# Token stage: the Silus of its input projection move into the scan stage, and its group norm's Silu becomes Exp and Ln

## The chip, the cores and the metric

The kernel runs on one core of a Trainium2 chip. The metric is the device time of one execution in microseconds (us), the median of several runs. The engines named are PE (TensorE, matmuls; its weight loads are shown apart as PEld), DVE (VectorE), ACT (ScalarE), POOL (GpSimd) and SP (SyncE, which here issues all DMA transfers). A line such as L470 is a line of the kernel's file before the change, unless the text says otherwise.

## The reference, cut to what matters

The input is a batch of 64 images of 128 channels and 28 x 28 pixels, f32. Four layers follow one another:

- a quantized block of two 3x3 convolutions with batch norms over the whole batch;
- an attention over the 784 pixels of each image;
- a state space layer ("mamba") along the 784 pixels of each image, with 160 inner channels and 24 states, whose result is fused into the image: this image is called x2 below;
- a second, small state space layer on each pixel alone: the 128 channels of a pixel are 8 tokens of 16, and the recurrence runs over the 8 tokens. A group norm over 4 groups of channels and a Silu follow, and x2 is added.

The last layer is what the change touches. Shortened:

```python
seq = x.transpose(0, 2, 3, 1).reshape(B * H * W, 8, 16)
xz = seq @ in_proj_w.T                          # 16 -> 2 * 32
xi, z = split(xz, 2)
xs = silu(conv1d(xi, conv_w) + conv_b)          # causal, over the tokens
dt, Bm, Cm = split(xs @ x_proj_w.T, [1, 17])
dt = softplus(dt @ dt_proj_w.T + dt_proj_b)
h_t = exp(dt_t * A) * h_{t-1} + dt_t * Bm_t * xs_t      # 8 steps, 32 x 16 states
y_t = sum over the states of h_t * Cm_t
y = (y + xs * D) * silu(z)
out = x + silu(groupnorm(y @ out_proj_w.T))
```

Both silu(conv1d(..)) and silu(z) depend on x2 of the pixel alone. Because the convolution over tokens is linear, in_proj and convolution together are one 128 x 256 matrix on the 128 channels (`wxc`, with `cbT` as bias), and z is another (`Wz`).

## The kernel before, in words

The kernel is written for a framework that orders the instructions of each engine ahead of time, by the order in which they are written and by its own estimate of when each can start. Each engine then runs its list in that order; semaphores between engines hold the data dependencies. When the activation table that ACT has in place does not hold the function of the next ACTIVATE, an ACT_TABLE_LOAD stands before it. Silu is in another table than Exp and Ln.

There are three stages.

The conv stage (`conv_block`) goes over the batch twice and leaves its result in DRAM.

The scan stage (`attention_and_mamba`) takes the images one by one. For image b, `scan` runs 30 steps (24 of part A, with all 128 partitions one channel each, and 6 of part B, with 32 channels and four states at a time). A step is: ACT's Exp gives `a` (L464); PE broadcasts a row of B over the partitions into `bc` (`product`, L240); DVE multiplies by it (L469), scans along the pixels (L470) and multiplies by the broadcast row of C (L473); PE sums into `y` (L475). `a` has three buffers, `bc` has two in PSUM, and `y` has one. Between the steps, `run` draws pieces of side work from the generator `beside`: first the end of image b-1 (`after`: output projection, the four copies that undo the permutation, L497 to L502, the fusion product and x2 at L507, which is stored into `x2d`), then the beginning of image b+1 (`before`: query, key, value, attention, layer norm, input projection, convolution, and delta). Each `yield` ends a piece. All products of side work use one PSUM buffer, `side`, of two banks (`side_psum`), so each waits until the one before has been read. The delta of the next image ends on POOL: L445, L446 and L448, which gives `du`, read by L469.

The token stage (`token_mamba`) takes groups of G = 14 times 128 pixels (28 groups; an image is 784 pixels, so a group holds 2.29 images). A group has two halves (`dh`, 16 inner channels each) and a half has four blocks of four channels. For a group:

- `silus(k)` loads x2 in chunks of up to 512 pixels (`xch`), multiplies by `wxc` and `Wz` (L679), applies Silu out of PSUM (the tile `s`, two buffers) and stores to `utd` and `ztd` in DRAM. `use` puts a table load before and one after. It is called for group k+1 in the second block of group k's first half, and for group 0 ahead of everything.
- `x_proj(k)` reads `utd` back (`rows`), multiplies (L706), and DVE copies the result to `BC` (L716); L723 and L726 form the sums over B times C.
- `delta_u(k, dh)` computes the softplus (ACT: Abs, Exp, Ln; DVE: L768 to L770; POOL: L773, L774) and, at L777, `diag`.
- `exps` makes the 64 Exps of a block, the tile `a` with two buffers, on ACT.
- `block` runs the recurrence: POOL makes the inputs (`inject`, L807) and two products (L818, L820); DVE makes the first sum (L819, into PSUM) and then, step by step, L822, L824 and L826; PE sums over the states (L829 to L833), and ACT copies the result to `ysb`.
- `gate` multiplies by silu(z) (DVE L849, POOL L850), projects (L858), and collects whole images in `xr` (L868).
- `image_stats` computes mean and variance of an image's groups of channels (L639 to L654), and `image_end` applies the Silu with scale and bias and adds x2 on POOL (L662). Since it is a Silu, it waits for the next call of `silus`, so that it shares its table.

ACT's activations of the token stage are all written through the helper `act` and show the line L609.

Of the kernel before, what the change touches and what calls it, by code (L numbers as in the profile page):

```python
# [15 lines left out]
F32 = mybir.dt.float32  # L16
# [25 lines left out]
PK4 = dict(Wz=256, BDx=512, BDt=16, BDo=256, dtw=32, dtb=32)  # L42
PK4_TMP = dict(P1=256, P2=256, Alog=512)
# [12 lines left out]
PK4_AT, NPK4 = columns(PK4)  # L56

# [9 lines left out]
def tile_kernel(ctx: ExitStack, tc: tile.TileContext, x, w1t, w2t, m2t, vecs, pk3, pk4, out):  # L67
# [18 lines left out]

    c2d, s2, b2x15 = conv_block(tc, cpool, dram, x, w1t, w2t, m2t, v, eps)
    attention_and_mamba(tc, x, c2d, s2, b2x15, x2d, pk3, vec, v, ident, eps)
    token_mamba(tc, x2d, pk4, v, ident, eps, out, NB)
# [117 lines left out]
def attention_and_mamba(tc, x, c2d, s2, b2x15, x2d, pk3, vec, v, ident, eps):  # L207
# [6 lines left out]
    with ExitStack() as ctx:  # L214
# [41 lines left out]
        nc.vector.tensor_copy(inb[:32, 3:4], inb_ps[:32, 0, 3:4])  # L256

# [228 lines left out]
        def after(b, given, ys):  # L486
# [21 lines left out]
            nc.sync.dma_start(x2d[b], x2)  # L508

# [25 lines left out]
        for _ in after(NB - 1, given.pop(NB - 1), ys):  # L535
            pass


def token_mamba(tc, x2d, pk4, v, ident, eps, out, NB):
# [14 lines left out]
    SET = "natural_log_exp_and_others"  # L554
# [3 lines left out]
    with ExitStack() as ctx:  # L558
        dram = ctx.enter_context(dram)
        wp = ctx.enter_context(tc.tile_pool(name="w4", bufs=1))  # L560
        wxc = wp.tile([C, 256], F32, name="wxc")
# [3 lines left out]
        with tc.tile_pool(name="w4t", bufs=1) as tp:  # L565

            pt = tp.tile([C, 1024], F32, name="pt")
            nc.sync.dma_start(pt, pk4[:, NPK4:])
            nc.vector.tensor_mul(wxc, pt[:, 0:256], pt[:, 256:512])
            nc.scalar.activation(A, pt[:, 512:1024], AF.Exp)  # L570
            nc.vector.tensor_scalar(A, A, -1.0, None, ALU.mult)
# [21 lines left out]

        utd = [dram.tile([C, 2, PX], F32, name=f"utd{i}") for i in range(2)]
        ztd = [dram.tile([C, 2, PX], F32, name=f"ztd{i}") for i in range(2)]
# [3 lines left out]
        side = dict(load=None, since=[])  # L599

        def behind(ins, others):
            for o in others:
                tc.add_manual_dep(
                    ins.ins, o.ins.name,
                    mybir.DependencyInfo(mybir.DependencyClass.NoSync, mybir.DependencyReason.DATA), reason="table",
                )

        def act(*args, **kw):
            ins = nc.scalar.activation(*args, **kw)  # L609
            if args[2] in (AF.Exp, AF.Ln, AF.Silu):  # L610
                if side["load"] is not None:
                    behind(ins, [side["load"]])
                side["since"].append(ins)

        def use(name):
            ins = nc.scalar.preload_act_table_set(name)
            behind(ins, side["since"] or [side["load"]] if side["load"] is not None else side["since"])
            side["load"], side["since"] = ins, []
# [4 lines left out]
        def load_x(k, g, n):  # L623

            lo, hi = k * PX + g * C, k * PX + (g + n) * C
            xch = cp.tile([C, 512], F32, name="xch", bufs=2)
            for b in range(lo // T, (hi - 1) // T + 1):
                p, q = max(lo, b * T), min(hi, (b + 1) * T)
                nc.sync.dma_start(xch[:, p - lo : q - lo], x2d[b][:, p - b * T : q - b * T])
            return xch  # L630

        xr, done = {}, []
        affine = {}

        def image_stats(b):
            xo = xr[b]
# [18 lines left out]
            affine[b] = sm  # L655

        def image_end(b):
            xo, sm = xr.pop(b), affine.pop(b)
            res = p1.tile([C, T], F32, name="res")
            nc.sync.dma_start(res, x2d[b])  # L660
            act(xo, xo, AF.Silu, bias=sm[:, 7:8], scale=sm[:, 5:6])
            nc.gpsimd.tensor_tensor(res, res, xo, ALU.add)  # L662
            nc.sync.dma_start(out[b], res)

        def silus(k):

            use("silu_and_others")
            for b in done:
                image_end(b)
            done.clear()  # L670
            if k >= NGRP:
                return
            for g, n in chunks:
                m = n * C
                xch = load_x(k, g, n)
                for dst, weight, bias in ((utd, wxc, "cbT"), (ztd, w("Wz"), None)):
                    for dh in range(2):
                        acc = bank()
                        nc.tensor.matmul(  # L679
                            acc[:, :m], lhsT=weight[:, dh * C : (dh + 1) * C], rhs=xch[:, :m], start=True, stop=True  # L680
                        )
                        s = cp.tile([C, 512], F32, name="s", bufs=2)
                        act(s[:, :m], acc[:, :m], AF.Silu, **(dict(bias=v(bias, dh)) if bias else {}))
                        nc.sync.dma_start(dst[k % 2][:, dh, g * C : g * C + m], s[:, :m])

        def load_rows(src, k, dh, g, n):
            t = cp.tile([C, 512], F32, name="rows", bufs=4)
# [203 lines left out]
        for q, (k, dh) in enumerate(halves_):  # L891
# [4 lines left out]
            for i in range(NBLK):  # L896

                take(ends, 2)
                if dh == 0:
                    if i == 1:  # L900
                        take(ends, 9)
                    elif i > 1:
                        take(group_next, 3)
# [115 lines left out]
```

## Time and profile before

The median of 3 runs is 19954.88 us (19948.64 to 19957.86); the profiled execution has a span of 19946.5 us.

| | busy us in the span | share |
|---|---|---|
| PE | 15221.5 | 76% |
| DVE | 15317.0 | 77% |
| ACT | 10216.1 | 51% |
| POOL | 6488.5 | 33% |

The page counts an f32 matmul as two matmul instructions. The scan stage runs from about 1100 us to 12860 us, the token stage's first block starts at 12970.3 us. A wait is written as the instruction that waited and, after the arrow, the instruction that ended the wait. An engine's idle time only costs where something waits for that engine in turn.

The rows of the page that the change removes, moves or has a likeness for:

| row | count | mean ns |
|---|---|---|
| L679 PE, products of `silus` | 896 | 592 to 627 |
| L609 ACT, the Silus `s`, with and without bias | 448 | 629 and 543 |
| L616 ACT table load | 59 | 1283 |
| L716 DVE, copies to `BC` | 196 | 692 |
| L609 ACT, Silu of the group norm on 784 elements | 64 | 1038 |
| L662 POOL, sum with x2, 784 elements | 64 | 1852 |
| L464 ACT, Exp of a scan step | 1920 | 947 |
| L284 ACT, Silu of z in the scan stage | 128 | 908 |
| L443, L376 ACT, Ln and Exp from SBUF, 784 elements | 128, 64 | 857 |
| L470 DVE, scan | 1920 | 1930 |

### The profile page before, as it was taken

What the parts mean: (1) busy time and instruction counts of PE and PEld (TensorE: products, weight loads), DVE (VectorE), ACT (ScalarE), POOL (GpSimd) and SP (SyncE); (2) the same over time, 40 slices, a digit from 0 to 9 for tenths busy, and PEclk for the clock granted to TensorE, in tenths of its full rate; (3) what the DMA queues carried; (4) which work ended last, traced back from release to release, by engine and by line L of the source; (5) the groups of instructions that cost most, each with busy time, mean ns of one, the idle gap of its engine ahead of it and who ended that gap; (6) DMA issues with size and microseconds to landing.
All of it is one profiled execution on the core that took longest, in us unless ns stands there. A gap on an engine that the chain in (4) does not pass through costs nothing.

```text
span 19946.5 us, 166453 instructions
## 1 busy us (share of the span) xinstructions
PE 15221.5 (76%) x56424; PEld 8635.8 (43%) x56424; DVE 15317.0 (77%) x15223; ACT 10216.1 (51%) x22804; POOL 6488.5 (33%) x3000
## 2 busy tenths in 40 slices
PE   9978888888888887888888888666666666666666
PEld 5533333333333333333333333355555555555554
DVE  1367877787787778878778787688888888888887
ACT  0234444444444444444444443377777777777776
POOL 0010110111011011101101100177777777777776
PEclk9988888888888888888888888888888888888888
DMA  2400000000000000000000000011111111111111
GB/s 75 146 7 7 6 8 7 7 7 7 8 6 8 7 6 8 7 8 6 8 7 6 8 5 3 23 55 62 64 64 62 64 62 65 62 63 64 62 64 53
DMA packets 325636, 631.19 MB, mean 32 GB/s; under 512 B 39856, under 2 KB 103856, under 8 KB 324784
## 3 DMA queue, kind: packets, MB, share of 16 engines
q1 hardware_dynamic: 324784, 620.55, 9.5%
q8 instruction: 447, 7.32, 0.2%
q14 instruction: 405, 3.32, 0.1%
HBM read 389.20 MB, written 231.21 MB: 31 GB/s over the span
## 4 chain that ended last, share of the span: by engine, by line
PE 44%; DVE 30%; ACT 10%; POOL 9%; issue 6%; DMA 2%; SPq 0%; DVEq 0%; POOLq 0%; ACTq 0%
PE side L240 13%; PE y L475 10%; DVE h L470 8%; PE y L831 5%; PE acc L120 5%; ACT a L609 4%; DVE h L473 4%; POOL db L807 4%; PE side L340 4%; DVE h L469 3%; PE bc L240 2%; DVE h L822 2%; DVE a L824 2%; DVE h L826 2%; DVE cv L392 2%
## 5 line engine op out<-in xcount | busy, mean ns | idle before, releaser
L609 ACT ACTIVATE a<-delta,A 128x98 f32<-128x98 f32 x14336 | 3891.9, 366 | 822.4 <-PE y L831 687.4
L470 DVE TENSOR_TENSOR_SCAN h<-a,h 128x784 f32<-128x784 f32 x1920 | 3706.1, 1930 | 43.9
L807 POOL TENSOR_TENSOR db<-u,BC 128x896 f32<-128x896 f32 x1568 | 3285.5, 2109 | 774.4 <-DVE h L826 664.8
L464 ACT ACTIVATE a<-delta,A 128x784 f32<-128x784 f32 x1920 | 1818.6, 947 | 3125.4 <-DVE h L470 3047.3
L475 PE MATMUL y<-h,ident 128*128 128x392 f32 x6144 | 2879.6, 595 | 629.4 <-DVE h L473 623.3
L831 PE MATMUL y<-a,ident 128*128 128x280 f32 x7168 | 2157.9, 462 | 1453.5 <-DVE a L824 1449.1
L378 POOL TENSOR_TENSOR xn<-xc,lnv 128x784 f32<-128x784 f32 x64 | 124.1, 1938 | 8617.9 <-ACT lnv L376 8617.9
L831 PEld LDWEIGHTS y<-a,ident 128*128 128x128 f32 x7168 | 1576.9, 224 | 2020.8 <-POOL db L807 1145.5
L473 DVE TENSOR_TENSOR h<-h,bc 128x784 f32<-128x784 f32 x1920 | 1852.6, 965 | 335.5 <-PE bc L240 310.9
L240 PE MATMUL bc<-parts,sel 128*128 128x392 bf16 x7680 | 1946.9, 377 | 190.4 <-DVE h L469 190.1
L475 PEld LDWEIGHTS y<-h,ident 128*128 128x128 f32 x6144 | 1218.1, 219 | 1693.4 <-DVE h L473 990.5
L469 DVE TENSOR_TENSOR h<-du,bc 128x784 f32<-128x784 f32 x1920 | 1850.0, 964 | 32.9 <-PE bc L240 24.5
L240 PEld LDWEIGHTS <-sel 128*128 128x128 bf16 x7680 | 776.3, 110 | 1815.2 <-issue 1531.8
L822 DVE TENSOR_TENSOR h<-h,a 128x896 f32<-128x896 f32 x1344 | 1474.4, 1097 | 37.4
L826 DVE TENSOR_TENSOR h<-h,db 128x896 f32<-128x896 f32 x1120 | 1229.2, 1097 | 62.3 <-POOL db L807 0.9
L475 PE MATMUL y<-h,fold 128*32 128x392 f32 x1536 | 748.6, 621 | 448.8 <-DVE h L473 448.8
L824 DVE TENSOR_TENSOR a<-h,BC 128x896 f32<-128x896 f32 x896 | 975.7, 1089 | 24.6
L340 PE MATMUL side<-diag,e 112*112 112x112 f32 x6272 | 807.2, 288 | 155.7 <-DVE diag L335 155.7
L328 DVE TENSOR_REDUCE nmax<-side 112x1 f32<-112x784 f32 x448 | 436.7, 975 | 631.9 <-PE side L240 631.9
L340 PEld LDWEIGHTS side<-diag,e 112*112 112x112 f32 x6272 | 798.7, 204 | 271.2 <-issue 228.2
L833 PEld LDWEIGHTS y<-late,ident 128*128 128x128 f32 x7168 | 848.4, 193 | 48.9 <-issue 28.5
L833 PE MATMUL y<-late,ident 128*128 128x112 f32 x7168 | 845.0, 274 | 0.0
(194 smaller groups left out, 22390.3 us busy)
## 6 DMA issues: line engine op xcount, KB each, us to landing
rows<-utd SPq DMA_DIRECT2D x504, 256.0 KB, 2.8
utd<-s SPq DMA_DIRECT2D x168, 256.0 KB, 2.9
ztd<-s SPq DMA_DIRECT2D x168, 256.0 KB, 2.9
rows<-ztd SPq DMA_DIRECT2D x168, 256.0 KB, 2.9
xt<-in_x SPq DMA_DIRECT2D x32, 784.0 KB, 5.1
c1d<-raw SPq DMA_DIRECT2D x32, 784.0 KB, 6.2
xt<-c1d SPq DMA_DIRECT2D x32, 784.0 KB, 6.0
c2d<-raw SPq DMA_DIRECT2D x64, 392.0 KB, 4.4
```

Source lines behind the costliest of these rows:

```text
L240: nc.tensor.matmul(dst[:, h, :HT], lhsT=lhsT, rhs=rhs[:, h * HT : (h + 1) * HT], start=(i == 0), stop=(i == len(terms) - 1),)
L340: nc.tensor.matmul(tr[:, j // 4, (j % 4) * TP : (j % 4 + 1) * TP], lhsT=e[:, j * TP : (j + 1) * TP], rhs=diag, start=True, stop=True,)
L464: nc.scalar.activation(a, deltas[i], AF.Exp, scale=A[:, k : k + 1])
L469: nc.vector.tensor_tensor(halves(h), halves(dus[i]), bb[:, :, :HT], ALU.mult)
L470: nc.vector.tensor_tensor_scan(h, a, h, 0.0, ALU.mult, ALU.add)
L473: nc.vector.tensor_tensor(halves(h), halves(h), cc[:, :, :HT], ALU.mult)
L475: nc.tensor.matmul(y[:, hf, :HT], lhsT=red, rhs=h[:, hf * HT : (hf + 1) * HT], start=(j == 0), stop=(j == count - 1),)
L609: ins = nc.scalar.activation(*args, **kw)
L807: nc.gpsimd.tensor_tensor(x, of_dg(du[:, t, ds, :]), BC[:, t, :NS, :].unsqueeze(1).broadcast_to([C, DB, NS, G]), ALU.mult)
L822: nc.vector.tensor_tensor(h, h, flat(at(t)), ALU.mult)
L831: nc.tensor.matmul(y3[:, 1:6], lhsT=ident, rhs=a[:, 0:5, :, n, :], start=False, stop=False)
L833: nc.tensor.matmul(y3[:, 6:8], lhsT=ident, rhs=late[:, :, :, n, :], start=False, stop=(n == NS - 1))
```

## The change

The two products of the token stage's input projection, their Silus and the stores into `utd` and `ztd` are now done image by image in the scan stage: `after` appends them behind x2, as four products with one Silu and one store each, in two pieces that each end with a `yield`. `utd` and `ztd` become one DRAM tile for each image, and `load_rows` reads a chunk with one transfer, or with two where it crosses from one image to the next. `silus` and `load_x` are gone, and `x_proj` can read a group at any time.

The Silu of the group norm becomes Exp, Ln and Exp again: with v = scale * x + bias, silu(v) = v * exp(-ln(1 + exp(-v))). The three ACT instructions share the table with the others of the token stage. DVE computes v (one instruction), and POOL multiplies the two. It is now done in `finish_image`, in one go with the statistics and as a part of the generator `gate`, instead of at the next `silus`. The token stage thus keeps one table from its start: one load stands ahead of it. The draws of the pieces in the main loop change with it: the last block of a half now draws all of `gate` that is left, and `x_proj` of the next group is drawn by two pieces from the second block of the first half on, instead of by three from the third.

The core of the diff:

```diff
@@ attention_and_mamba, after
             nc.sync.dma_start(x2d[b], x2)
+            for dst, weight, bias in ((utd, wxc, "cbT"), (ztd, wz, None)):
+                for dh in range(2):
+                    acc = side_psum()
+                    product(acc, [(weight[:, dh * C : (dh + 1) * C], x2)])
+                    tok = tmp("tok")
+                    last[:] = [
+                        nc.scalar.activation(
+                            halves(tok), acc[:, :, :HT], AF.Silu, **(dict(bias=v(bias, dh)) if bias else {})
+                        )
+                    ]
+                    nc.sync.dma_start(dst[b][:, dh, :], tok)
+                yield
@@ token_mamba
-        def use(name):
-            ins = nc.scalar.preload_act_table_set(name)
...
+        load = nc.scalar.preload_act_table_set("natural_log_exp_and_others")
@@ finish_image (was image_stats and image_end)
+            nc.vector.tensor_scalar(sm[:, 0:1], sm[:, 5:6], -1.0, None, ALU.mult)
+            nc.vector.tensor_scalar(sm[:, 1:2], sm[:, 7:8], -1.0, None, ALU.mult)
             res = p1.tile([C, T], F32, name="res")
             nc.sync.dma_start(res, x2d[b])
-            act(xo, xo, AF.Silu, bias=sm[:, 7:8], scale=sm[:, 5:6])
+            e = p1.tile([C, T], F32, name="gate")
+            act(e, xo, AF.Exp, bias=sm[:, 1:2], scale=sm[:, 0:1])
+            act(e, e, AF.Ln, bias=1.0)
+            act(e, e, AF.Exp, scale=-1.0)
+            nc.vector.tensor_scalar(xo, xo, sm[:, 5:6], sm[:, 7:8], ALU.mult, ALU.add)
+            yield
+            nc.gpsimd.tensor_tensor(xo, xo, e, ALU.mult)
             nc.gpsimd.tensor_tensor(res, res, xo, ALU.add)
@@ load_rows
-            t = cp.tile([C, 512], F32, name="rows", bufs=4)
-            nc.sync.dma_start(t[:, : n * C], src[k % 2][:, dh, g * C : (g + n) * C])
+            t = cp.tile([C, 512], F32, name="rows", bufs=6)
+            for b in range(lo // T, (hi - 1) // T + 1):
+                p, q = max(lo, b * T), min(hi, (b + 1) * T)
+                nc.sync.dma_start(t[:, p - lo : q - lo], src[b][:, dh, p - b * T : q - b * T])
@@ main loop
                 take(ends, 2)
-                if dh == 0:
-                    if i == 1:
-                        take(ends, 9)
-                    elif i > 1:
-                        take(group_next, 3)
+                if i == NBLK - 1:
+                    take(ends, 99)
+                if dh == 0 and i > 0:
+                    take(group_next, 2)
                 take(nxt, 1)
...
-                if dh == 0 and i == 1:
-                    silus(k + 1)
-                    use(SET)
```

## The prediction

> **What bounds the kernel now.** I read first the span in slices (section 2 of the page), each digit the busy tenths of one 498.7 us slice. Up to slice 3 the conv stage runs, to slice 26 the scan stage, and from there the token stage.
>
> ```profile
> PE   9978888888888887888888888666666666666666
> DVE  1367877787787778878778787688888888888887
> ACT  0234444444444444444444443377777777777776
> POOL 0010110111011011101101100177777777777776
> ```
>
> No engine is full: the scan stage has PE and DVE near 8 tenths and ACT at 4; the token stage has DVE at 8, ACT and POOL at 7. Both stages are bound by waits in in-order queues. So I took one period of each, busy times by window (columns: window, length, then busy time of PE, PE loads, DVE, ACT, POOL):
>
> ```profile
> 6003.80:6188.40 184.60, 148.16 (x485) 69.73 (x484) 147.13 (x146) 77.17 (x95) 20.20 (x9) 0.87 0.02 7
> 15007.00:17010.00 2003.00, 1349.24 (x6290) 1039.93 (x6288) 1637.59 (x1579) 1458.36 (x4730) 1497.56 (x693) 0.83 0.20 63
> ```
>
> The first is one image of the scan stage: 184.6 us, DVE idle for 37. The second is some eight token groups. L723 runs once per group, from 12926.4 to 19551.7 us in 27 intervals: 245.4 us per group, so the 2003 us hold 8.16 groups. Per group that is DVE 200.7 busy and 44.7 idle, POOL 183.5, ACT 178.7, PE 165. What DVE waits for in 15000 to 17000 (total us, times, longest):
>
> ```profile
> DVE BC L716 <- PE bank L706: 182.2, 56, 10.5
> DVE h L819 <- POOL a L818: 75.8, 24, 6.9
> DVE xr L868 <- PE bank L858: 22.9, 12, 3.2
> ```
>
> Half of the idle time, 182.2 / 8.16 = 22.3 us per group, is one place. DVE's timeline there:
>
> ```profile
> 15031.70 1.09 DVE L824 TENSOR_TENSOR late<-h,BC 128x896 f32<-128x896 f32 x1
> 15039.99 0.69 DVE L716 COPY BC<-bank 128x512 f32<-128x512 f32 x1 [7.20 <-PE bank L706]
> ...
> 15058.99 0.69 DVE L716 COPY BC<-bank 128x512 f32<-128x512 f32 x1 [8.33 <-PE bank L706]
> ...
> 15061.73 3.91 DVE L777 TENSOR_TENSOR diag<-u,small 128x1792 f32<-128x1792 f32 x1
> 15065.56 2.82 DVE L819 TENSOR_TENSOR h<-a,db 128x896 f32<-128x896 f32 x1
> ```
>
> A block ends at 15032.8 and the next starts at 15065.6. ACT explains it:
>
> ```profile
> 15039.46 0.38 ACT L609 ACTIVATE s<-bank 128x256 f32<-128x256 f32 x1 [3.08 <-DMA utd<-s]
> 15039.86 1.28 ACT L616 ACT_TABLE_LOAD   x1
> 15041.16 1.70 ACT L609 ACTIVATE w<-w 128x1792 f32<-128x1792 f32 x1
> 15042.76 17.20 ACT L609 ACTIVATE a<-delta,A 128x98 f32<-128x98 f32 x64
> ```
>
> The 16 Silus of the next group stand together between two table loads, and their two buffers `s` wait for stores (99.2 + 54.3 us of ACT idle in these 2000 us, 18.8 per group). Only after the last may the 64 Exps of the next block run, 17.2 us, and the next group's x_proj (L706) cannot read `utd` before. The same delay returns as a wait of 6.88 us at the block at 15116.59 for POOL's L818, which waited for ACT's `a`.
>
> **What the skill says.** "ScalarE: Activation LUTs", section "What ACT_TABLE_LOAD costs": about 1283 ns and a drain of about 1380 ns. The trace has 1283 ns, and the next ACTIVATE starts 10 to 20 ns after; the drain is not seen apart, so I price a load at 1.28 us and take the page's 2.66 as the upper end. "PSUM — Partial Sum Buffer", section "Engine vs sequencer instructions": ScalarE, VectorE and GpSimd queues are strict FIFO and matmuls keep program order; the block waiting behind Silus agrees. "SBUF — State Buffer", section "SBUF: two separate sides": DVE instructions with two SBUF inputs and GpSimd instructions lock each other out; L819 (both inputs in SBUF) takes 1.10 us alone and 2.82 beside POOL, L470 1.79 and up to 3.48. So POOL work added to the token stage is not free for DVE.
>
> **The change, token stage.** Removed per group: 16 matmuls, 16 Silus, two loads, the `xch` reads and the `s` stores. In the changed program's DVE order the seven BC copies no longer stand in a row: they lie between operations of the group's last two blocks, with `rows` read from DRAM that the scan stage filled long before. The copies, L723 and diag (4.8 + 2.0 + 3.9 = 11 us of DVE) remain, the idle time between them has other work in it. I count off 22.3 us, and of the 9.3 per group at L819 the 6.9 after the Silus. ACT loses 16 x 0.58 + 2 x 1.28 = 12 us, which was beside DVE's work but for that gap.
>
> Added per image, 784 x 64 / 1792 = 2.29 images per group: Exp, Ln, Exp for one Silu of 1.04 us (rows of 857 ns for 784 elements: 2.6 us; net +1.6 ACT, hidden, since ACT has 178.7 - 12 + 3.6 = 170 of some 220 us); on DVE one 784 tensor_scalar (L296, same shape, 0.56) and two single-column ones (0.2 to 0.6, L653's 0.51 at the top): 1.0 x 2.29 = 2.2 us per group, on the path since DVE is the fullest; on POOL one product, 1.85 (L662): 4.2 us per group, making POOL 188. The new waits (DVE's affine behind ACT's first Exp; POOL's product behind Ln and Exp) I bound by 0 and by the ACT wait of the group norm today at three places, 3 x 1.7 x 2.29 = 12 us (L652 waits 1.7 at most); the order leaves several DVE operations between, so I take 3.
>
> Sum per group: -22.3 - 6.9 + 2.2 + 3 = -24, to 221.4; between -15 and -29. 27 groups have it: -650 us (-405 to -780). A check by blocks on the group that starts at 15065.56 and took 252.8 us, a long one: by the starts of L819, its four plain blocks take 22.3 to 24.7 us, the two with softplus 29.5 and 34.6, and the last two, with group norm, BC copies, L723 and diag added to 22.4 of block work, some 33 and 34: 226, or 27 less. silus(0) ran alone before the first block, 12887 to some 12920: -33.
>
> **The change, scan stage.** Added per image: 4 products of two f32 matmuls (the page counts each as two; one product 1.48 us in PE's timeline): 5.9 us PE; 4 Silus of 0.91. In the changed ACT order each stands alone between two `a` Exps, so each brings two loads: 4 x (2.57 + 0.91) = 13.9 us ACT. Program counts agree: 582 loads become 1021, 499 more after the token stage's 60 go. ACT had 77 of 184.6 us busy, so 91 fit. Behind a waiting Silu stand the `a` Exps, needed by DVE's scans (L470); behind a waiting product stand y and the bc broadcasts, because `side` has one buffer. Four stores per image, 1.6 MB, are some 9 GB/s.
>
> What moves: the products take one scan step each, directly after x2. Before, in the 50 us from the first delta product (6053.7) to the vt products (6104.0), four of image b's steps (B part) and four of b+1's lay; several were bare of side work, and DVE idled there:
>
> ```profile
> 6091.20 0.87 DVE L502 COPY r<-side 32x392 f32<-32x392 f32 x1 [5.41 <-ACT r L501]
> ```
>
> After, B's steps end some 3.5 earlier, eight of b+1's steps lie between, and the four new products fill them. I walked this stretch by the trace's durations in the new order. B's last y stands right behind the first delta product; then ACT's Abs, Exp, Ln with their loads and POOL's three products (L445, L446, L448: 1.84, 1.89 and 1.84 us at their shortest in this image) must end before DVE's first product of b+1: DVE idles 4 to 5 us, where before it idled 5.41 behind the yo product. The steps with a new product take 4.4 us by PE's chain (half y 0.74, product 1.48, half y 0.74, cc 0.42, DVE 0.97) against some 3.65 by DVE alone: four times 0.7. ACT needs 2.57 + 0.91 + 0.95 = 4.4 per such step and starts two `a` ahead: just hidden. Idle time thus stays about 11 us, vt comes 1 to 2 us later. Ends: -2 us per image (all in idle time and a shorter stretch before) and +5.9 (all PE work on the path). I take +1.5 x 63 = +95. The last image's four products have no scan beside them: 4 x 3.5 = 14 us.
>
> **Sum.** 19955 - 650 - 33 + 95 + 14 = 19381; I say 19380.
>
> **Rivals.** (1) ACT's table loads do reach DVE's scans, in full: +13.9 x 63 = 876 instead of 95: 20160, slower. For it: ACT's steps just fit, and side work is serial through one buffer. Against it: ACT waits 46.8 us per image for DVE's L470, that is, for buffers, not the reverse. (2) POOL becomes the token stage's bound: it is at 183.5 and gets 4.2 more, and near the end, with no side work, blocks still start 22.4 apart with 1.8 us waits for L818. If only 10 us per group are won: 19380 + 14 x 27 = 19760. (3) The products fill idle slots wholly and the stretch before shrinks: -2 x 63 in place of +95: 19160.
>
> **Numbers.** The forecast 0.64, (2) 0.14, (3) 0.12, (1) or half of it 0.10. The range takes (3) and the token bounds to 19100, and most of (2) to 19720. Faster by over 0.2% 0.88, within it 0.03, slower 0.09.
>
> **What would show it.** After: no table loads from some 13000 us on; no run of BC copies with waits on L706's successor; groups 215 to 230 us apart; DVE there at 9 tenths. Scan: 183 to 190 us per image, eight more loads in each, a wait of DVE for POOL's du at the image boundary. Wrong would be: images over 192 us with scans waiting for ACT's `a`, or groups over 235 with DVE waiting for POOL or for the group norm's Exp.

## The result and the profile after

The changed kernel takes 19391.79 us, median of 4 runs (19387.71 to 19407.3); the kernel before, in the same comparison, 19951.76 us. The ratio is 0.9724, with a 95% interval of 0.9707 to 0.974. The forecast was 19380 us, and the medians differ from it by only 12 us.

That closeness is luck: the total hides two misses of opposite sign and of the same size, 193 us each. The blocks gained 457 us where 650 were forecast, and the scan stage gained 98 where a loss of 95 was forecast. First and last starts of single lines cut the two profiled runs (spans 19946.5 and 19390.3 us) into stretches; the names of the lines are those of before, with the new line numbers after the stroke:

| stretch | before, us | after, us | difference | forecast |
|---|---|---|---|---|
| start to the first scan, L470 / L483 | 1116.6 | 1125.7 | +9 | 0 |
| first to last scan | 11740.2 | 11642.0 | -98 | +95 |
| last scan to last x2, L507 / L520 | 19.1 | 20.7 | +2 | 0 |
| last x2 to the first block, L819 / L811 | 94.4 | 80.5 | -14 | -33 + 14 = -19 |
| first to last block | 6904.5 | 6447.4 | -457 | -650 |
| last block to the end | 71.7 | 74.0 | +2 | 0 |

In the slices of the page after, a digit is again the busy tenths of one fortieth of the span:

```profile
PE   9978888888888888888888888866666666666666
DVE  1368878878788878888888887778888888888888
ACT  0235445445445445445445455457777777777776
POOL 0001101101101101101001011048888888888887
```

ACT in the scan stage went from 4 to between 4 and 5 tenths. In the token stage DVE now shows 8 throughout, where the forecast looked for 9, and POOL went to 8.

**Token stage.** L715 (was L723) runs from 12826.5 to 18981.7 us in 27 intervals: 228.0 us per group, from 245.4. The longest of DVE's waits between these two times (us in total, times, longest) follow; first of before, from 12926.9 to 19551.7 us:

```profile
DVE BC L716 <- PE bank L706: 618.3, 188, 13.8
DVE h L819 <- POOL a L818: 258.9, 78, 13.4
DVE xr L868 <- PE bank L858: 70.4, 38, 3.2
DVE yg L849 <- PE bank L844: 28.7, 26, 4.7
DVE yg L849 <- DMA rows<-utd: 6.1, 11, 2.0
```

and of after:

```profile
DVE h L811 <- POOL a L810: 233.0, 65, 13.4
DVE xr L860 <- PE bank L850: 184.3, 67, 6.4
DVE BC L708 <- PE bank L698: 62.5, 57, 2.0
DVE yg L841 <- PE bank L836: 60.2, 26, 5.0
DVE yg L841 <- DMA rows<-utd: 26.4, 21, 3.7
```

Divided by 27, the wait of the BC copies fell from 22.9 to 2.3 us per group, as forecast. The wait at the start of a block hardly fell: 9.6 to 8.6. Two others grew: the copy into `xr` from 2.6 to 6.8, and the gate's `yg` from 1.3 to 3.2 (for PE and for `rows` from DRAM together). In all, DVE's idle time fell by 17.9 us per group and its busy time rose by 0.5.

**Scan stage.** Some rows of the same list, from the first x2 to the last (63 images); of before:

```profile
DVE r L502 <- ACT r L501: 337.4, 64, 7.3
DVE h L473 <- PE bc L240: 306.0, 393, 6.7
DVE rest L422 <- ACT parts L421: 166.5, 62, 3.6
DVE cv L390 <- ACT xm L388: 140.2, 60, 2.4
```

and of after:

```profile
DVE h L486 <- PE bc L244: 332.1, 451, 9.0
DVE h L482 <- POOL du L461: 217.5, 62, 4.1
DVE cv L403 <- ACT xm L401: 205.8, 62, 4.0
DVE vt L329 <- PE side L323: 64.9, 62, 1.1
DVE rest L435 <- ACT parts L434: 48.4, 58, 0.8
DVE r L515 <- ACT r L514: 31.6, 55, 8.9
```

Per image, the wait of the copy `r` fell by 4.9 us and that of `rest` by 1.9; the new wait for POOL's du costs 3.5. Smaller changes nearly cancel: `cv`, `vt` and `dt` wait 2.6 us more, and two rows that the list leaves out, of the attention's maxima and of the softplus' `pos`, 2.0 less. The windows give DVE's share as a whole (window, length, busy time of PE, PE loads, DVE, ACT, POOL, each with its instructions, then TensorE's clock, the DMA's share and GB/s); before:

```profile
1309.60:12875.90 11566.30, 9321.39 (x30240) 4314.26 (x30238) 9208.15 (x9129) 4816.37 (x5924) 1251.05 (x560) 0.87 0.02 7
```

and after:

```profile
1321.80:12788.40 11466.60, 9400.43 (x31248) 4366.89 (x31246) 9204.98 (x9129) 5674.88 (x6673) 1131.71 (x560) 0.88 0.04 15
```

DVE has the same work, 9208 and 9205 us, so the gain is idle time: 2358 to 2262, or 1.5 us per image. The 98 us are clear of the scatter: the kernels below that keep the order of before in this stage on all four engines (b_s7, a_noprod, a_noprod2) take 11727.5 to 11746.8 us for it, and those that keep the order of after (a_gnsilu, a_db6, g_u) 11625.2 to 11645.4. ACT has 858 us more, and it costs DVE nothing that shows here. ACT's timeline in one image:

```profile
6071.85 1.28 ACT L528 ACT_TABLE_LOAD   x1
6073.15 0.91 ACT L528 ACTIVATE tok<-side,vec 128x784 f32<-128x784 f32 x1
6074.08 1.28 ACT L477 ACT_TABLE_LOAD   x1
6075.37 0.95 ACT L477 ACTIVATE a<-delta,A 128x784 f32<-128x784 f32 x1
6076.34 1.28 ACT L528 ACT_TABLE_LOAD   x1
```

Load, Silu, load, Exp fill 4.49 us from one load to the next of its kind, without a gap. DVE's scans in the same stretch start 3.9 to 4.6 us apart, and DVE waited for ACT's `a` in the whole scan stage once, for 0.5 us. The last column of the rows of L483 and L477 (idle before, and what ended it) says the same: `a` waits for DVE, 2040 us of it, not DVE for `a`.

```profile
L483 DVE TENSOR_TENSOR_SCAN h<-a,h 128x784 f32<-128x784 f32 x1920 | 3502.2, 1824 | 66.5 <-DVE h L482 0.9 <-ACT a L477 0.5
L477 ACT ACTIVATE a<-delta,A 128x784 f32<-128x784 f32 x1920 | 1810.9, 946 | 2102.2 <-DVE h L483 2040.5 <-POOL delta L459 53.3
```

### The profile page after: what moved, and what is told of

Same layout as the page of the kernel before. It is cut to its first block, busy times and chain, and to the rows that moved or that the text cites. A ratio compares the mean times of both kernels' runs of the same rounds, so it can differ in the third digit from the quotient of the medians.

```text
span 19390.3 us, 167002 instructions
## 1 busy us (share of the span) xinstructions
PE 15010.2 (77%) x56552; PEld 8571.3 (44%) x56552; DVE 15343.1 (79%) x15415; ACT 10844.4 (56%) x23179; POOL 6488.9 (33%) x3064
## 4 chain that ended last, share of the span: by engine, by line
PE 45%; DVE 26%; ACT 13%; POOL 10%; issue 6%; DMA 1%; SPq 0%; DVEq 0%; POOLq 0%; ACTq 0%
PE side L244 13%; PE y L488 12%; ACT a L627 5%; PE acc L124 5%; DVE h L486 5%; DVE h L483 4%; PE y L823 4%; POOL db L799 4%; PE side L353 4%; PE bc L244 3%; DVE h L482 2%; DVE h L814 2%; DVE a L816 2%; DVE h L818 2%; DVE cv L405 2%
## 5 line engine op out<-in xcount | busy, mean ns | idle before, releaser
L503 POOL TENSOR_TENSOR yo<-yo,z 128x784 f32<-128x784 f32 (+1 forms) x128 | 243.6, 1903 | 10035.4 <-DVE yo L493 10035.4
L799 POOL TENSOR_TENSOR db<-u,BC 128x896 f32<-128x896 f32 x1568 | 3332.4, 2141 | 741.6 <-DVE h L818 600.0
L483 DVE TENSOR_TENSOR_SCAN h<-a,h 128x784 f32<-128x784 f32 x1920 | 3502.2, 1824 | 66.5 <-DVE h L482 0.9
L477 ACT ACTIVATE a<-delta,A 128x784 f32<-128x784 f32 x1920 | 1810.9, 946 | 2102.2 <-DVE h L483 2040.5
L244 PE MATMUL bc<-parts,sel 128*128 128x392 bf16 x7680 | 1878.8, 365 | 314.7 <-DVE h L482 312.1
L482 DVE TENSOR_TENSOR h<-du,bc 128x784 f32<-128x784 f32 x1920 | 1847.2, 962 | 251.0 <-POOL du L461 221.9
L818 DVE TENSOR_TENSOR h<-h,db 128x896 f32<-128x896 f32 x1120 | 1227.5, 1096 | 50.4 <-DVE late L816 0.5
L816 DVE TENSOR_TENSOR a<-h,BC 128x896 f32<-128x896 f32 x896 | 974.3, 1087 | 20.6
L353 PE MATMUL side<-diag,e 112*112 112x112 f32 x6272 | 747.1, 274 | 163.5 <-DVE diag L348 163.5
L353 PEld LDWEIGHTS side<-diag,e 112*112 112x112 f32 x6272 | 739.8, 191 | 279.2 <-issue 236.5
L344 ACT ACTIVATE e<-side,nmax 112x784 f32<-112x784 f32 x448 | 409.6, 914 | 778.5 <-DVE nmax L341 778.5
```

The source lines that it names most:

```text
L244: nc.tensor.matmul(dst[:, h, :HT], lhsT=lhsT, rhs=rhs[:, h * HT : (h + 1) * HT], start=(i == 0), stop=(i == len(terms) - 1),)
L353: nc.tensor.matmul(tr[:, j // 4, (j % 4) * TP : (j % 4 + 1) * TP], lhsT=e[:, j * TP : (j + 1) * TP], rhs=diag, start=True, stop=True,)
L477: nc.scalar.activation(a, deltas[i], AF.Exp, scale=A[:, k : k + 1])
L482: nc.vector.tensor_tensor(halves(h), halves(dus[i]), bb[:, :, :HT], ALU.mult)
L483: nc.vector.tensor_tensor_scan(h, a, h, 0.0, ALU.mult, ALU.add)
L799: nc.gpsimd.tensor_tensor(x, of_dg(du[:, t, ds, :]), BC[:, t, :NS, :].unsqueeze(1).broadcast_to([C, DB, NS, G]), ALU.mult)
```

## The experiments

Each ratio is to the kernel before in the same comparison. Scan stage and group period are measured as in the table above; before has 11740.2 and 245.4 us, after 11642.0 and 228.0.

**b_s7.** The kernel before, with seven shared buffers for `s` and `rows`, so that the Silus need not wait for their stores.

```diff
-                        s = cp.tile([C, 512], F32, name="s", bufs=2)
+                        s = cp.tile([C, 512], F32, name="s", tag="rows", bufs=7)
...
-            t = cp.tile([C, 512], F32, name="rows", bufs=4)
+            t = cp.tile([C, 512], F32, name="rows", tag="rows", bufs=7)
```

> The kernel before, with the Silus' staging tile s in one pool of seven buffers together with rows (before: two for s, four for rows), so that the Silus no longer wait for their own stores. Nothing else is changed. Theory A (the gap between blocks is the whole bundle: Silus, table loads and x_proj behind them, and waiting for stores is only a part of it): some 8 us per group are won of the 17 that the change brought, ratio to before 0.987 to 0.993, and DVE still waits 10 us or more per group in front of the BC copies. Theory B (the two buffers were the fault, the place of the Silus was not): the 18.8 us per group of ACT waiting for stores go, the BC gap closes, ratio 0.974 to 0.980, about what the whole change gives.

Measured: 19709.27 us, ratio 0.9886 (0.9871 to 0.99); 236.6 us per group, 8.8 fewer. DVE's waits from 12926.9 to 19300 us:

```profile
DVE BC L716 <- PE bank L706: 387.7, 156, 9.7
DVE h L819 <- POOL a L818: 254.8, 68, 13.4
DVE diag L777 <- POOL u L774: 138.5, 11, 16.7
```

The wait of the BC copies fell from 22.9 to 14.4 us per group while the Silus and both loads stayed. So a good third of that gap was the two buffers. The rest goes with the place of the Silus in the order, ahead of what the copies need: ACT's wait for the stores fell from 19.0 to 0.9 us per group, but the Silus now wait 8.3 us for their products (L679), where it was 2.2. The wait at the start of a block did not fall in sum, and `diag` now waits 5.1 us per group for POOL's `u`.

**a_gnsilu.** The changed kernel with the group norm's Silu back, once per group between two table loads; the projection stays in the scan stage. It takes the group norm's part out of the change, and draws all of `gate` in one more place, the second block of the first half. The core of the edit:

```diff
+        def silus():
+            use("silu_and_others")
+            for b in sorted(done):
+                image_end(b)
+            done.clear()
...
-            e = p1.tile([C, T], F32, name="gate")
-            act(e, xo, AF.Exp, bias=sm[:, 1:2], scale=sm[:, 0:1])
-            act(e, e, AF.Ln, bias=1.0)
-            act(e, e, AF.Exp, scale=-1.0)
-            nc.vector.tensor_scalar(xo, xo, sm[:, 5:6], sm[:, 7:8], ALU.mult, ALU.add)
-            yield
-            nc.gpsimd.tensor_tensor(xo, xo, e, ALU.mult)
+            act(xo, xo, AF.Silu, bias=sm[:, 7:8], scale=sm[:, 5:6])
```

> The changed kernel with the group norm's Silu back as a Silu: the images of a group are collected and closed together, between two table loads, in the second block of the next group's first half. The input projection stays in the scan stage. Theory A (what counts in the token stage is where the projection's Silus and products stand; table loads are 1.28 us each and hidden): within 0.4% of the changed kernel, ratio to before 0.969 to 0.976. Theory C (the gain comes from having no table switch in the token stage): 54 loads and the waits around them come back, ratio 0.980 or more. The prediction's price of the new group norm, 2.2 to 5 us per group, would show as a gain of 60 to 140 us.

Measured: 19238.13 us, ratio 0.9648 (0.9632 to 0.9664), faster than both kernels. 222.5 us per group; the scan stage, 11645 us, is that of after. The 52 loads in the token stage cost 66.7 us of ACT's time, beside other work. So the three-step Silu costs 5.5 us per group (3.7 of DVE's busy time and 1.8 of its idle time), and moving the projection away, with the buffers and draws that go with it, brings 22.9. The waits between the first and last group:

```profile
DVE h L820 <- POOL a L819: 256.1, 59, 13.4
DVE xr L869 <- PE bank L859: 151.0, 62, 5.7
```

The wait at the block's start is again 9.5 us per group. The starts of all blocks show where it sits. A group is counted here from one L723 (L715, L724) to the next, and the average is over the groups with eight blocks between them (us per group):

| wait of a block's first sum for POOL's `a` | 3rd block | 4th | 5th | 6th | all eight |
|---|---|---|---|---|---|
| before | 5.3 | 1.1 | 0.8 | 2.0 | 9.4 |
| after | 0 | 4.7 | 0 | 2.9 | 8.4 |
| a_gnsilu | 0 | 5.7 | 0 | 2.9 | 9.3 |

(The second and first block make up the sums.) In before, the third block is the one whose Exps come after the Silus. That wait is gone entirely, and another stands at the fourth block. POOL's `a` at the blocks' starts (L818, L810) waited 9.1 us per group for ACT's Exps in before and 0.5 in after, so the Exps are no longer the reason. In b_s7 the same happened with the Silus still in the token stage: the block that waited in before does not wait, and the next one waits 5.5 us per group. In after, ahead of one of these, POOL did this:

```profile
15329.55 4.85 POOL L765 TENSOR_TENSOR delta<-delta,w 128x1792 f32<-128x1792 f32 x1
...
15336.26 3.98 POOL L766 TENSOR_TENSOR u<-delta,u 128x1792 f32<-128x1792 f32 x1
15340.21 2.08 POOL L812 TENSOR_TENSOR a<-a,BC 128x896 f32<-128x896 f32 x1
15342.25 11.44 POOL L799 TENSOR_TENSOR db<-u,BC 128x896 f32<-128x896 f32 x6
15353.60 2.13 POOL L810 TENSOR_TENSOR a<-a,db 128x896 f32<-128x896 f32 x1
```

and DVE, right after it:

```profile
15355.76 1.10 DVE L811 TENSOR_TENSOR h<-a,db 128x896 f32<-128x896 f32 x1 [5.72 <-POOL a L810]
```

POOL has next to no gap from 15329.55 on: the softplus' `delta` and `u`, 8.8 us, stand in its queue, and the inputs of two blocks come late. In before, the two kinds of groups exclude each other: of 26, 21 wait 5.8 to 7.3 us at the third block and not at all at the fourth; in the other 5 the softplus stands one block earlier in the queues, the third block does not wait, and the fourth waits 5.6 or 5.7 us for just this queue of POOL's. From the first block's start to the fifth's, the two kinds take 104.7 and 104.2 us on the mean, so the missing wait at the third block gained next to nothing there.

**a_ident.** The changed kernel with Identity for the four Silus, which leaves the Silu of both projections out; Identity stands without a load of its own here, and the loads at L528 and two thirds of those at L477 go, 8 per image.

```diff
-                            halves(tok), acc[:, :, :HT], AF.Silu, **(dict(bias=v(bias, dh)) if bias else {})
+                            halves(tok), acc[:, :, :HT], AF.Identity, **(dict(bias=v(bias, dh)) if bias else {})
```

> The changed kernel with Identity in place of the four new Silus per image, so that xs and z enter without their Silu; products, stores and places stay, and the eight added table loads per image go, 10.3 us of ACT per image. Theory A (the loads are hidden behind DVE and PE in the scan stage): scan stage within 1 us per image of the changed kernel's, ratio to before 0.968 to 0.973. Rival (loads delay the Exps a or hold up the side buffer): 3 to 10 us per image less, ratio 0.94 to 0.963.

Measured: 19869.26 us, ratio 0.9966 (0.9953 to 0.9979). The scan stage got longer, to 12121.4 us or 192 per image, with less work. The scheduler had drawn a different order: the new products now stood close together ahead of the steps, not one in each, and DVE waited for other things:

```profile
DVE h L482 <- PE bc L244: 516.5, 199, 5.6
DVE h L486 <- PE bc L244: 265.9, 329, 2.2
DVE w L454 <- ACT ab L452: 196.5, 61, 3.3
DVE r L515 <- ACT r L514: 177.3, 118, 8.8
```

So this run does not price the loads. It shows how much an order can be worth: 479 us between two orders, the longer one with less work.

**a_noprod.** No new products and Silus: x2 itself is stored four times. It leaves out both projections and their Silus.

```diff
-                    acc = side_psum()
-                    product(acc, [(weight[:, dh * C : (dh + 1) * C], x2)])
-                    tok = tmp("tok")
-                    last[:] = [
...
-                    ]
-                    nc.sync.dma_start(dst[b][:, dh, :], tok)
-                yield
+                    nc.sync.dma_start(dst[b][:, dh, :], x2)
```

> The changed kernel without the four new products and Silus per image: x2 itself is stored four times in their place, so projection and Silu are left out of the result, and the token stage is as in the changed kernel. It shows what the new pieces cost the scan stage. Theory A1 (they lie in idle slots and, by moving the end of the old image against the start of the next, shorten the stage themselves): the scan stage is as long as before the change, some 184 us per image, ratio to before 0.974 to 0.979, slower than the changed kernel or equal. Theory A2 (they cost something, and the shorter scan stage has another cause): 2 to 6 us per image less than the changed kernel, ratio 0.953 to 0.967.

Measured: 19689.85 us, ratio 0.9874 (0.9859 to 0.9888). The scan stage is 11740.3 us, that of before to 0.1 us, and the order of its instructions on PE, DVE, ACT and POOL is that of before throughout. So taking the new work out of the scan stage does not shorten it below after's; it loses the gain. The token stage, 234.3 us per group, had an accident: the single table load was tied behind the Silus that are no longer there, and 366 loads stood between its Exps and other functions:

```profile
L618 ACT ACT_TABLE_LOAD x366 | 469.6, 1283 | 392.8 <-PE y L814 372.4 <-DVE h L802 14.9
```

**a_noprod2.** The same, with that load tied behind the copies `r`.

```diff
-                nc.scalar.copy(r_hw[64:96, h * 14 : (h + 1) * 14], half[64:96])
+                last[:] = [nc.scalar.copy(r_hw[64:96, h * 14 : (h + 1) * 14], half[64:96])]
```

> The run a_noprod again (the changed kernel, x2 stored four times in place of the four products and Silus, which are left out of the result), with the token stage's one table load tied behind the last image's copies r. In a_noprod it was tied to nothing, and the token stage had 366 table loads. Scan stage as before the change (11740 us), token groups as in the changed kernel (228 us apart): the sum is 98 us more than the changed kernel, ratio to before 0.975 to 0.980. If the token groups stay at 234 us, the loads were not the cause: 0.984 or more.

Measured: 19477.5 us, ratio 0.9764 (0.9749 to 0.9779); scan stage 11727.5, groups 228.1. The token half of the change alone gives the group period of after, so the two halves add. The 366 loads of the run before had cost 6.2 us per group. Table loads are thus not free everywhere: there, DVE's steps of the group norm's statistics waited 222.0 us for ACT's `sm`, where after has 30.4.

**a_identp1.** Identity again, with a `yield` on both sides of each product, so that each has a piece of its own. The theory was that a_ident was slow because its products stood together. It leaves the same Silu out.

```diff
                 for dh in range(2):
+                    yield
                     acc = side_psum()
...
-                yield
+                    yield
```

> The changed kernel with Identity in place of the four new Silus per image (xs and z enter without their Silu) and with a yield before and after each new product, which puts the products again into different scan steps, as in the changed kernel, and not in a bunch as in the run a_ident. Eight table loads per image fewer than the changed kernel. Theory A (the place of the products sets the length of the scan stage; the loads are hidden on ACT): scan stage within 1.5 us per image of the changed kernel's 184.8, ratio to before 0.967 to 0.977. Rival (the fewer loads themselves made a_ident slow or the loads cost time): it stays near a_ident's 192 us per image, ratio 0.99 or more, or falls below 181, ratio under 0.962.

Measured: 19890.58 us, ratio 0.9972 (0.9962 to 0.9982), scan stage 12138 us. The theory fell: with the products apart, the stage is as long as in a_ident. DVE's longest wait in the scan stage:

```profile
DVE r L515 <- ACT r L514: 615.6, 62, 10.6
```

It is 9.9 us per image at the copies `r`, where after has 0.5. This wait lies at the image boundary, ahead of the products. It is not the wait that a_ident had most of, so what made that run slow stays open.

**b_holdbc.** The kernel before, with the pieces of the next image from the bc products on held back until the 30 scan steps are done. No product is added, no Silu moved.

```diff
             bc = []
-            yield
+            yield "hold"
...
+            held = []
+
             def run(n):
                 for _ in range(n):
-                    next(steps, None)
+                    if not held and next(steps, None):
+                        held.append(b)
```

> The kernel before, without anything of the change; only the pieces of side work from the B and C rows of the next image on (bc, then delta) are held back until the 30 scan steps of the present image are written. That puts the next image's delta behind the last steps of part B, as in the changed kernel: its chain over ACT and GpSimd and the old image's chain over yo and the copies r then run side by side and not one after the other. Theory F (the changed kernel's shorter scan stage comes from this order at the image boundary, not from the new products): DVE's wait for r (5.3 us per image) falls under 1.5, a wait for du of 2 to 5 us appears, scan stage 0.5 to 4 us per image shorter, ratio to before 0.987 to 0.998. Rival G (with no products to fill them, the scan steps that then lie bare cost as much as is won): 0.998 or more.

Measured: 19772.4 us, ratio 0.9914 (0.9899 to 0.9929). The scan stage is 11558 us, 182 shorter than before and 84 shorter than after. The wait of `r`, 337 us before, fell to 10.5; other waits now read:

```profile
DVE w L441 <- ACT ab L439: 188.2, 57, 3.3
DVE h L469 <- PE bc L240: 146.6, 136, 2.0
DVE x L507 <- PE side L240: 79.2, 62, 2.0
```

A wait for POOL's du, which had been expected as the price, hardly appeared: 24.0 us in the whole stage. That detail missed; the theory that order at the boundary alone shortens the stage held. The order is not that of after, though, so the run shows that such an order can be worth more than the change's gain, and not how that gain is made up.

**a_db6.** The changed kernel with six buffers `db` in place of five, so that POOL can make inputs further ahead; A is computed in place to make room (not shown).

```diff
-        db = ctx.enter_context(tc.tile_pool(name="db4", bufs=5))
+        db = ctx.enter_context(tc.tile_pool(name="db4", bufs=6))
```

> The changed kernel with six instead of five buffers for the inputs db that GpSimd makes for the recurrence (the room comes from computing A in place). Theory D (DVE's remaining wait of 8.6 us per group for L810 at the start of a block is GpSimd held back by full buffers: 571 us of its waits are for L818 to free one): the wait falls by 3 us per group or more, ratio to before 0.964 to 0.970. Theory E (GpSimd's own work at the turn from block to block is the limit, a buffer more does not help): within 0.2% of the changed kernel, ratio 0.971 to 0.974.

Measured: 19385.09 us, ratio 0.9719 (0.9704 to 0.9733), 228.3 us per group. No effect: full buffers did not hold POOL back here. Whether it is late with its queue is tested by g_u below.

**a_pos.** The changed kernel with the first of the three products that end in du moved from POOL to DVE for part A, to shorten the wait for du.

```diff
-                nc.gpsimd.tensor_tensor(pos, pos, ab, ALU.subtract)
+                (nc.vector if i == 0 else nc.gpsimd).tensor_tensor(pos, pos, ab, ALU.subtract)
```

> The changed kernel with one of the three GpSimd products that end the delta of part A (L458, the subtraction) on VectorE. Theory A (at the image boundary DVE waits 3.5 us per image for du, the end of a chain through ACT and GpSimd, and GpSimd beside it slows DVE's L454 from 0.6 to 1.5 us): the wait falls by about 1.5 us per image, scan stage 1 to 2.5 us per image shorter, ratio to before 0.964 to 0.970. Rival (the stage is bound by PE and the side buffer, and the wait for du only moves): within 0.2% of the changed kernel, 0.970 to 0.975.

Measured: 19507.3 us, ratio 0.9782 (0.9766 to 0.9799); scan stage 11754.6. The wait for du fell from 217.5 to 120.6 us, and the order of `r` and the new products changed with it: waits for `bc` (146.2 us at L482) and x2 (74.7) came in, and DVE, which now does the product, is busy for 44 us more. The intended effect was reached and the stage got longer.

**best7.** a_gnsilu with a_pos's edit, seven buffers `db`, and A computed in place to make room for them.

> The pieces put together: the changed kernel, the group norm's Silu as a Silu once per group between two table loads (run a_gnsilu, 0.9648), L458's product of part A on VectorE, and seven buffers db. If the three are independent and theories A and D hold, 0.953 to 0.962; if neither of the two new pieces helps, 0.963 to 0.967.

Measured: 19363.53 us, ratio 0.9709 (0.9695 to 0.9724); groups 222.7, scan stage 11755.7. The buffers bring nothing, and a_pos's order costs 110 us.

**g_u.** a_gnsilu with `u` of the first half, one of the two softplus products in POOL's queue, on DVE.

```diff
-            nc.gpsimd.tensor_tensor(u_, v_, u_, ALU.mult)
+            (nc.vector if dh == 0 else nc.gpsimd).tensor_tensor(u_, v_, u_, ALU.mult)
```

> The run a_gnsilu with the product delta times u (4.2 us on GpSimd for 1792 elements) of one half of each group on VectorE, the half after whose softplus DVE waits 5.7 us for L810's counterpart at the next block. Theory H (this wait, which the prediction gave to the Silus, is GpSimd's own queue: delta and u, 8.8 us, stand between its inputs for the blocks): DVE's wait for GpSimd at the block starts falls from 9.5 us per group by 3 us or more, DVE gets 1.9 to 2.5 us more, together 1 to 2.5 us per group less, ratio to before 0.961 to 0.9645. Rival (the wait has another cause, as ACT's Exps): it stays, and the time is the same or 0.3% more, 0.9645 to 0.968.

Measured: 19466.63 us, ratio 0.9759 (0.9742 to 0.9775); 230.9 us per group. DVE's waits from 13000 to 18800 us:

```profile
DVE h L820 <- POOL a L819: 166.8, 57, 4.4
DVE u L775 <- POOL delta L774: 138.5, 25, 5.8
```

The first was 240.8 in a_gnsilu over the same time; at the fourth block it fell from 5.7 to 2.3 us per group. So POOL's queue is what the fourth block waits for. But DVE now waits in its own queue for POOL's `delta`, and has the product to do as well: its idle time rose by 2.6 us per group and its busy time by 5.8. The wait was moved, not removed.

**g_hold.** a_gnsilu with the two delta pieces of the next image held back until the scan's steps are done.

```diff
+            yield "hold"
             deltas, dus = [], []
...
-                    next(steps, None)
+                    if not held and next(steps, None):
+                        held.append(b)
```

> The version with the group norm's Silu once per group (19238 us, scan stage 11645 us, groups 222.5 us), and of the side work the two delta pieces of the next image alone are held back until the 30 scan steps are done. Theory F (the order at the image boundary sets the length of the scan stage, and VectorE still waits there): VectorE's waits behind r and at the last sums of part B go, and the scan stage falls by 1 to 3 us per image, 60 to 190 us: 19050 to 19180 us. Rival: in this order part B's last steps already stand ahead of most of the delta work, and holding it back only starts GpSimd's three products later: VectorE's wait for du grows from 3.5 us per image to 6 or more and the scan stage gets longer by 2 to 5 us per image, 19360 to 19550 us. The token stage stays at 222 to 223 us per group in both cases.

Measured: 19243.96 us, ratio 0.9644 (0.9628 to 0.966); scan stage 11656 us, against 11645. Neither theory's number came: the wait for du is 225.8 us, about that of after. From the third image on, the order of instructions is the one without the hold: this part of the order at the boundary was already as the hold makes it.

## Why the prediction was right, step by step

- **Token stage, BC copies, -22.3 us per group: right.** Measured -20.6. b_s7 confirms one half of the named cause, Silus waiting for their stores, with 8.5 us; the other half, copies behind Silus, agrees with the rest of the gap.
- **Token stage, -6.9 of the 9.3 at L819: failed.** The prediction said "I count off 22.3 us, and of the 9.3 per group at L819 the 6.9 after the Silus." The block of 15116.59 was read rightly: the third block's wait, 5.3 per group, is gone. But the fourth block now waits for POOL's softplus products, 4.7 per group, and the sum fell by 1.0. The prediction took the block's wait as ending when ACT's Exps come, and put the queue of POOL, which ends second there, at nothing; g_u shows that this queue is the cause. The 5 groups of before without a wait at the third block already showed this, since they were only 0.5 us faster up to the fifth block; the step rested on one group of the other kind.
- **New group norm, +2.2 of DVE and +3 of waits: right as a sum, not in its parts.** a_gnsilu prices it at 5.5. The three new DVE instructions take 2.3 us per group, as forecast. The 3 us did not come as waits of DVE: its wait in the statistics (L652, L656) fell from 1.6 to 1.1. What grew is the busy time of the statistics' other single-column steps, by 3.0, beside POOL (last section), and POOL itself waits 2.7 us for the last Exp. That DVE's busy time rose by only 0.5 over all is because other instructions got shorter: `diag`, the softplus' steps and the blocks' first sums, by 2.8.
- **Not in the sum.** The copies `xr` wait 4.2 us per group more and `yg` 1.9 more, 0.8 of it for `rows` from DRAM. The last block of a half now draws all of `gate` at once, which would pack these; that is argued, and no run tests it. Over all, -17.4 us per group, near the lower end of the range from -15 to -29, so -457 us and not -650 over the blocks.
- **Scan stage, +1.5 us per image: failed in sign.** Of its parts, the wait for du came nearly as forecast (4 to 5 us, measured 3.5), the wait for `r` went (5.4, measured 4.9), the steps with a product take about 4.3 us in the image shown (forecast 4.4), and DVE does not wait for ACT's loads. The failed step is the choice between the two ends: "-2 us per image (all in idle time and a shorter stretch before) and +5.9 (all PE work on the path). I take +1.5". Measured is -1.5, at the lower end. The walk ended at vt and left out what the new order changes elsewhere: 1.9 us less at `rest`, and the smaller changes at `cv`, `dt` and the maxima. The "shorter stretch before" was the larger matter: b_holdbc gets 2.9 us per image from the order there with nothing moved, and a_noprod, which takes the products out and so returns to the order of before, loses the gain.
- **Last image and first Silus, -19: right,** measured -14.
- **Rivals.** (1), loads that reach the scans through `a`, is out: 0.5 us in the whole stage. (3), products in idle slots and a shorter stretch before, agrees with the scan stage: it has -126 us, and -98 were measured. (2), POOL as the token stage's bound, holds in part: its queue takes the place of a removed wait, while its total, 5016 us of 6155, is not the bound.

So the total came out right because two errors cancelled: the token stage missed 193 us through a wait that was replaced and through new waits at the gate, and the scan stage gave as much through an order that was priced too low.

What stays open: the price of the table loads with the order held fixed, since every variant without them was given another order; what the change's new draws and its six buffers `rows` do in the token stage apart from the moved projection; and how much of the scan stage's -98 us would be more without the new products in that same order.

## What to carry to other kernels

Price a removed wait by what comes second at the same place, and look for it in repeats of the pattern where the first was absent. Where queues are ordered by a scheduler, an edit at a boundary changes the order, and that can count for more than its added work: here 2.9 us per image for order alone, against no visible wait of the scans for eight table loads. So compare the order of the instructions before reading a variant's time. If one function needs another table, gathering its uses can be cheaper than building it from three others: once per group, with two loads, it was 222.5 against 228.0 us here.

## What the runs showed of the hardware

- **DVE beside POOL.** In the scan stage the scan fell from 1930 to 1824 ns, mean of 1920, while L441's successor L454 rose from 628 to 1471 and L442's, L455, from 958 to 1237. The work moved in time against POOL's softplus products, which took 2345 to 2490 ns each before and 1846 to 2552 after. The Trainium skill, "SBUF — State Buffer", section "SBUF: two separate sides", says that a DVE instruction with two SBUF inputs and a GpSimd instruction exclude each other for the whole instruction. The scan has two such inputs, `a` and `h`, and agrees: in after, the 1781 scans that overlap no POOL instruction take 1776 to 1793 ns, and the 139 that do take 2267 on the mean. The total of DVE's busy time did not move (9208 and 9205 us), so for DVE contention was shifted and not saved; POOL's busy time fell from 1251 to 1132 us.
- **Single columns beside POOL.** The group norm's statistics have DVE instructions on 128 x 1 elements. In after, those of L650 to L658 that overlap no POOL instruction take 163 ns on the mean, those that do 974. They cost 4.9 us per group before and 7.9 after.
- **Silu out of PSUM.** With a bias per partition it takes 914 ns, without one 824, on the same 784 elements:

```profile
L528 ACT ACTIVATE tok<-side,vec 128x784 f32<-128x784 f32 x128 | 117.0, 914 | 38.7 <-PE side L244 37.9
L528 ACT ACTIVATE tok<-side 128x784 f32<-128x784 f32 x128 | 105.5, 824 | 5.8 <-PE side L244 4.4
```
